# A two-layer graph kernel whose instructions are issued in a second hand-fixed order

## Chip, core and metric

The kernel runs on one core of one Trainium2 chip. The metric is the device time of one launch in microseconds (us). The core has engines that run side by side and each take their instructions in order: PE (TensorE, the matrix products; PEld is its weight load), DVE (VectorE), ACT (ScalarE), POOL (GpSimd) and SP (SyncE, which here issues all transfers). Products land in PSUM, everything else lives in SBUF.

## What is computed

There are 64 independent graphs of 256 nodes with 256 features, each with a 256x256 integer adjacency matrix. Each goes through two layers. Cut to what matters:

```python
# layer 0: attention with 8 heads of 32, masked by relation r = 0..3
q, k = src @ Wq + bq, src @ Wk + bk
attn = softmax(einsum('bhid,bhjd->bhij', q, k) / sqrt(dh))
for r in range(4):
    out += einsum('bhij,bhjd->bhid', attn * (adj == r), src @ Wv[r] + bv[r])
x = ln(src + out @ Wo + bo)
x = ln(x + gelu(x @ W1 + b1) @ W2 + b2)
# layer 1: two graph-attention products, then a feed-forward part
def gat(h, W, a):
    Wh = h @ W
    e = leaky_relu(Wh @ a[:F] + (Wh @ a[F:]).T)
    return softmax(where(adj > 0, e, NEG), axis=1) @ Wh
h = ln(x + gat(gat(x, gW1, ga1), gW2, ga2))
return ln(h + relu(h @ w_ff1 + b_ff1) @ w_ff2 + b_ff2)
```

All products are in f32.

## The kernel before

One graph is cut into 203 named steps. `operations` of the class Graph returns them as a table from name to function. A table `PLACES` gives each name a number; step n of graph g stands at g * PERIOD + PLACES[n], with PERIOD = 60. At the end of the kernel all steps of all graphs are put in one list, sorted by that number, and issued in that order (lines 678 to 690):

```python
plan += [(g * PERIOD + t, i, ops[n]) for i, (n, t) in enumerate(PLACES.items())]
...
for _, _, f in sorted(plan, key=lambda p: p[:2]):
    f()
```

So the numbers are not times. They only set in which order each engine gets its instructions. Since a graph's places stretch over some 408, seven graphs are in flight at a time: while one graph's scores are made, an older one is in its feed-forward part. The 49 remaining weight loads stand at PLACES["jT"] + 3 i (LOAD_STEP), and three pieces that prepare weights at FFA_PLACE, GAT_PLACE and FFB_PLACE.

The steps of a graph, with their engines (m is the half of the heads, 0 or 1; h the head in it; c or the last digit a half of the nodes or a part):

- SP: `load` (features and adjacency), `jT` (transposing load), `eW`/`eR` (softmax weights of one head written to DRAM and read back transposed), `aW`/`aR`, `hW`/`hR`, `bW`/`bR` (the same for the input of the first feed-forward part, of the graph attention, of the second feed-forward part), `y` (residual), `store`.
- PE: `qk0 qk1` (queries and keys), `s0 s1` (scores: 32-row products, four on the array side by side), `v00 v01 v10 v11` (values for four relations), `po0 po1` (masked weights times values: 32-column products, four side by side), `wo`, `au0..3` and `ad0..7` (first feed-forward part up and down), `ga0 ga1`, `ipA ipB` (short products that spread a column), `h10 h11`, `h2`, `bu0..3` and `bd0..7` (second feed-forward part).
- ACT: `qkc` (copy of queries and keys), `exp`, `nrm`, `ec` (copy of a head's weights into PSUM), `oT` (copy of po), `ax` (gelu after au), `bx` (relu after bu), `ln`, `gac`, `zA zB`, `zeA zeB`, `h1c`.
- DVE: `xT`, `max`, `rec`, `vc` (v plus bias), `eT`, `pm` (three relations' masks times weights), `ya`, `aT`, `hT`, `bT`, `ae`, `be`, `st`, `nb`, `zl zm zx zd`, `h2a`.
- POOL: `cast`, `mask0..4`, `pl` (mask of the last relation times weights), `rt`, `ag ar bg br`, `lg lb`, `yb`.

Buffers go by tags. `qk`, `v`, `po`, `wo`, `au`, `bu`, `ga`, `ip`, `h1` and `h2` all take their PSUM tile from the tag mm with two buffers (lines 109 and 116), the down products and `ec` have one buffer each (line 111), and each head of `s` has one (line 110). `pm` and `pl` have four buffers, an eT read three.

In the middle of the run the order of one period is, on PE (cyclic; steps of five graphs):

```
ad2 ad3 ad4 ad5 ad6 ad7 qk1 po1 s0 v10 wo bu0 bu1 bu2 bu3 v11 bd0 ga0 ga1 bd1 ipA
bd2 v00 bd3 bd4 bd5 po0 s1 h10 h11 au0 ipB bd6 bd7 au1 v01 au2 ad0 ad1 au3 h2 qk0
```

on ACT:

```
ec13 nrm03 exp13 qkc0 exp11 ln3 exp10 nrm11 ec02 qkc1 nrm13 oT1 ec01 ln2 nrm12 ec00 bx0
bx1 ln4 bx2 nrm10 exp02 bx3 ln1 ec03 gac0 gac1 ec11 zA exp01 exp03 exp00 nrm02 zeA oT0
nrm01 h1c0 h1c1 zB ax0 ec10 ax1 zeB ax2 ec12 nrm00 ax3 exp12
```

and on SP:

```
store jT eW01 eW00 eR01 eR00 bW bR y load eW03 eR03 hW hR eW11 eR11 aW aR eW12 eR12 eW10
eR10 eW13 eW02 eR13 eR02
```

Of the kernel before, what the change touches and what calls it, by code (L numbers as in the profile page):

```python
# [25 lines left out]

PERIOD = 60.0
PLACES = {
    "load": 12.69, "cast": 34.43, "xT": 36.95, "qk0": 57.08, "jT": 61.53, "qkc0": 62.55, "qk1": 67.8,
    "qkc1": 70.21, "s0": 70.47, "max02": 72.23, "exp02": 81.06, "max01": 82.27, "max03": 86.02,  # L30
    "max00": 88.95, "rec02": 89.87, "exp01": 91.67, "v00": 92.06, "exp03": 92.94, "rec03": 93.5,
    "exp00": 93.85, "nrm02": 93.87, "s1": 95.88, "mask0": 96.09, "rec01": 96.51, "rec00": 97.66,
    "vc00": 97.9, "nrm01": 98.6, "eT02": 98.81, "mask1": 101.7, "max12": 103.23, "eW02": 104.42,
    "v01": 106.53, "max13": 109.53, "eT01": 110.69, "vc01": 112.14, "mask4": 115.25, "nrm00": 115.76,
    "mask2": 116.32, "exp12": 117.58, "eR02": 118.03, "max11": 118.71, "nrm03": 120.47, "eW01": 121.68,
    "exp13": 121.99, "eT00": 122.41, "eW00": 123.28, "max10": 123.96, "eT03": 124.13, "exp11": 124.37,
    "eR01": 124.69, "rec11": 124.91, "exp10": 125.28, "nrm11": 125.32, "rec12": 125.99, "rec13": 126.63,
    "ec02": 126.77, "eR00": 126.89, "eT11": 128.18, "y": 130.66, "nrm13": 131.27, "v10": 131.71,
    "pm02": 131.73, "ec01": 132.85, "mask3": 132.88, "pl02": 133.27, "vc10": 133.65, "pm01": 133.94,
    "nrm12": 134.13, "ec00": 134.17, "rec10": 134.86, "eW03": 135.24, "pl00": 135.39, "eT12": 136.41,  # L40
    "eR03": 136.43, "eW11": 138.29, "pl01": 138.69, "pm00": 140.86, "nrm10": 140.96, "v11": 141.16,
    "vc11": 142.32, "eR11": 143.59, "ec03": 145.79, "pm03": 145.85, "eT10": 146.5, "eT13": 148.99,
    "eW12": 150.09, "ec11": 150.62, "pl03": 151.26, "eR12": 152.59, "po0": 155.58, "oT0": 157.09,
    "eW10": 157.11, "pm11": 157.99, "eR10": 160.55, "eW13": 162.85, "pl11": 163.84, "ec10": 166,
    "pm10": 170.09, "pl10": 170.24, "ec12": 172.37, "yb": 172.85, "eR13": 175.34, "pm12": 178.71,
    "pl12": 179.18, "ec13": 180.43, "pm13": 182.8, "pl13": 184.21, "po1": 189.19, "oT1": 192.18,
    "wo": 192.72, "ya": 194.55, "st1": 197.35, "rt1": 197.54, "nb1": 201.83, "ln1": 203.94, "aT": 203.97,
    "aW": 208.22, "aR": 209.8, "au0": 219.72, "ax0": 225.43, "au1": 226, "ag": 226, "ar": 226.9,
    "ax1": 227.05, "au2": 229.76, "ad0": 230.11, "ax2": 231.84, "ad1": 233.09, "au3": 233.11, "ax3": 236.44,
    "ad2": 240.24, "ad3": 240.48, "ad4": 240.68, "ad5": 240.9, "ad6": 241.73, "ad7": 243.34, "ae": 247.23,  # L50
    "st2": 247.9, "rt2": 249.32, "nb2": 252.05, "ln2": 253.74, "lg2": 255.16, "lb2": 255.29, "hT": 255.42,
    "hW": 256.6, "hR": 258.07, "ga0": 265.07, "ga1": 265.22, "gac0": 266.18, "gac1": 267.17, "ipA": 268.92,
    "zA": 270.83, "zlA": 271.44, "zmA": 272.81, "zxA": 274.65, "zeA": 276.11, "zdA": 277.61, "h10": 278.15,
    "h1c0": 279.36, "h11": 279.54, "h1c1": 279.92, "ipB": 280.31, "zB": 281.13, "zlB": 281.58,
    "zmB": 283.67, "zxB": 284.08, "zeB": 290.21, "zdB": 293.16, "h2": 293.21, "h2a": 300.38, "st3": 301.14,
    "rt3": 303.61, "nb3": 304, "ln3": 304.93, "bT": 306.81, "bW": 308.89, "bR": 309.2, "bu0": 314.34,
    "bu1": 315.21, "bx0": 315.73, "bx1": 317.62, "bu2": 318.08, "bu3": 318.55, "bx2": 318.88, "bx3": 322.44,
    "bd0": 324.24, "bd1": 327.98, "bd2": 330.87, "bd3": 332.25, "bd4": 332.79, "bd5": 333.36, "bg": 335.88,
    "bd6": 340.88, "br": 341.18, "bd7": 342.49, "be": 349.69, "st4": 354.87, "rt4": 359.05, "nb4": 373.16,
    "ln4": 378.29, "lg4": 386.9, "lb4": 395.75, "store": 420.32,  # L60
}
LOAD_STEP = 3.0
FFA_PLACE, GAT_PLACE, FFB_PLACE = 195.0, 200.0, 255.0

# [653 lines left out]
```

## Time and profile before

| what | us |
|---|---|
| median of 3 runs | 3654.48 (3651.39 to 3654.7) |
| the profiled execution | 3653.86 |
| its span, first to last instruction | 3652.1 |
| PE busy in the span | 3567.7 |
| transfers, share of the DMA engines' time | 42.5% |

A matmul record's duration reaches past the start of the next record, since products are pipelined. What a product costs PE is therefore read from the starts of two records in a row, and a wait shows where a row of the timeline carries an idle time and a releaser in square brackets. Every f32 product shows as two records; so a step like au0 (two blocks, each summed over two halves) has eight. Names in the profile are those of tiles: ffa_ps is au, ffa_po is ad, ffb_ps is bu, ffb_po is bd, ga_wps is ga, ga_ips and gb_ips are ipA and ipB, h_ps is h1 and h2.

### The profile page before, as it was taken

The page shows a single profiled execution, that of the slowest core. Times are in us where ns is not written, and L with a number is a line of the kernel's source. Part 1 is how long each engine was busy: PE and PEld are TensorE (multiplying, and loading weights), DVE is VectorE, ACT ScalarE, POOL GpSimd, SP SyncE. Part 2 cuts the span into 40 slices and gives each one's busy share as a digit, 9 for nine tenths or more (in the row PEclk, how much of TensorE's full clock was granted, in tenths as well). Part 3 has the DMA queues.
Part 4 walks back from the last instruction along what each step waited for, and adds up shares of the span by engine and source line. Part 5 has one row for each costly group of instructions (what it writes and reads, how often), then busy time and mean ns, then how long its engine had stood idle before and what let it go on. Part 6 is the DMA issues. An engine that isn't in the chain of part 4 may idle for free.

```text
span 3652.1 us, 65487 instructions
## 1 busy us (share of the span) xinstructions
PE 3567.7 (98%) x22872; PEld 2712.3 (74%) x22872; DVE 2703.1 (74%) x5132; ACT 2630.4 (72%) x6787; POOL 2012.5 (55%) x1734
## 2 busy tenths in 40 slices
PE   6899999999999999999999999999999999999996
PEld 3677777777777777777777777777777777777775
DVE  5777777777777777777777777777777777777762
ACT  4677777777777777777777777677677677777763
POOL 3455555555555555655655655655655655555552
PEclk8999999999999999999999999999999999999998
DMA  7444444444444444444444444444444444444430
GB/s 186 123 128 126 123 135 125 122 132 125 128 128 128 128 126 124 131 125 128 128 127 125 128 129 123 132 126 126 132 125 124 133 124 124 131 126 124 129 96 26
DMA packets 809850, 457.46 MB, mean 125 GB/s; under 512 B 334256, under 2 KB 718896, under 8 KB 809520
## 3 DMA queue, kind: packets, MB, share of 16 engines
q1 hardware_dynamic: 809520, 453.27, 42.5%
q8 instruction: 181, 2.97, 0.4%
q14 instruction: 149, 1.22, 0.1%
HBM read 243.42 MB, written 201.33 MB: 122 GB/s over the span
## 4 chain that ended last, share of the span: by engine, by line
PE 94%; DMA 3%; DVE 1%; ACT 1%; SPq 1%; issue 0%; POOL 0%; POOLq 0%; ACTq 0%; DVEq 0%
PE po L504 12%; PE ffb_ps L349 12%; PE ffb_po L363 12%; PE ffa_ps L349 12%; PE v_ps L436 12%; PE ffa_po L363 12%; PE qk_ps L417 6%; PE s L452 4%; PE h_ps L583 3%; PE ga_wps L534 3%; PE h_ps L597 3%; PE wo_ps L524 3%; DMA eT_d<-eT_sq 1%; DMA hT<-hT_d 0%; PE gb_ips L546 0%
## 5 line engine op out<-in xcount | busy, mean ns | idle before, releaser
L487 DVE TENSOR_TENSOR pm<-rel,pe 128x1536 f32<-128x1536 uint8 x512 | 890.1, 1739 | 137.2 <-PE po L504 118.8
L492 POOL TENSOR_TENSOR pl<-rell,eT 128x512 f32<-128x512 bf16 x512 | 596.4, 1165 | 513.3 <-PE po L504 398.3
L318 POOL TENSOR_TENSOR rs_x<-ve_x,nhalf 128x2 f32<-128x2 f32 x256 | 180.2, 704 | 976.0 <-DVE ve_x L314 686.2
L436 PE MATMUL v_ps<-wv,xT 128*128 128x512 f32 x1024 | 493.2, 604 | 4.5 <-DVE v L443 3.6
L363 PE MATMUL ffb_po<-f,ffb_h 128*128 128x256 f32 x2048 | 493.5, 379 | 0.0
L349 PE MATMUL ffa_ps<-ffa_T,w 128*128 128x256 f32 x2048 | 483.9, 379 | 3.5 <-ACT ffa_h L356 2.5
L465 ACT ACTIVATE e<-s,nmax 128x256 f32<-128x256 f32 x1024 | 474.4, 483 | 3.9 <-DVE nmax L457 1.9
L349 PE MATMUL ffb_ps<-ffb_T,f 128*128 128x256 f32 x2048 | 458.0, 382 | 16.0 <-DMA ffb_T<-ffb_T_d 16.0
L483 ACT COPY pe<-eT 128x512 f32<-128x512 f32 x512 | 306.8, 599 | 227.2 <-DVE pm L487 166.6
L475 ACT ACTIVATE e<-e,rden 128x256 f32<-128x256 f32 x1024 | 466.4, 512 | 0.9 <-DVE rden L470 0.9
L363 PE MATMUL ffa_po<-w,ffa_h 128*128 128x256 f32 x2048 | 462.9, 379 | 0.0
L363 PEld LDWEIGHTS ffb_po<-f,ffb_h 128*128 128x128 f32 x2048 | 379.7, 190 | 98.1 <-issue 57.8
L349 PEld LDWEIGHTS ffa_ps<-ffa_T,w 128*128 128x128 f32 x2048 | 388.9, 190 | 84.1 <-ACT ffa_h L356 18.0
L349 PEld LDWEIGHTS ffb_ps<-ffb_T,f 128*128 128x128 f32 x2048 | 393.0, 192 | 71.4 <-issue 12.4
L443 DVE TENSOR_TENSOR v<-v_ps,bv_r 128x512 f32<-128x512 f32 x256 | 174.3, 681 | 349.0 <-PE v_ps L436 218.4
L363 PEld LDWEIGHTS ffa_po<-w,ffa_h 128*128 128x128 f32 x2048 | 389.5, 190 | 52.5
L269 DVE STREAM_TRANSPOSE eT_sq<-e 128x512 f32<-128x512 f32 x512 | 357.5, 698 | 19.4 <-DMA eT_d<-eT_sq 10.8
L504 PE MATMUL po<-pm,v 128*32 128x256 f32 x6144 | 361.2, 383 | 10.5 <-DVE pm L487 6.5
L457 DVE TENSOR_REDUCE nmax<-s 128x2 f32<-128x512 f32 x512 | 345.1, 675 | 6.2 <-PE s L452 6.2
L504 PEld LDWEIGHTS po<-pm,v 128*32 128x32 f32 x6144 | 187.3, 110 | 167.6 <-ACT pe L483 19.9
L436 PEld LDWEIGHTS v_ps<-wv,xT 128*128 128x128 f32 x1024 | 188.1, 191 | 165.9 <-issue 146.4
L356 ACT ACTIVATE ffb_h<-ffb_ps,bf_c 128x256 f32<-128x256 f32 x512 | 215.0, 473 | 109.4 <-PE ffb_ps L349 109.3
(109 smaller groups left out, 5964.9 us busy)
## 6 DMA issues: line engine op xcount, KB each, us to landing
eT_d<-eT_sq SPq DMA_DIRECT2D x512, 256.0 KB, 3.2
eT<-eT_d SPq DMA_DIRECT2D x512, 256.0 KB, 2.9
xin<-in_x_dram SPq DMA_DIRECT2D x256, 64.0 KB, 3.0
adi<-in_adj_dram SPq DMA_DIRECT2D x64, 256.0 KB, 3.4
y<-in_x_dram SPq DMA_DIRECT2D x64, 256.0 KB, 3.4
ffa_T_d<-ffa_T_sq SPq DMA_DIRECT2D x64, 256.0 KB, 2.4
ffa_T<-ffa_T_d SPq DMA_DIRECT2D x64, 256.0 KB, 3.0
hT_d<-hT_sq SPq DMA_DIRECT2D x64, 256.0 KB, 2.4
```

The lines of the kernel that those rows point to most:

```text
L269: nc.vector.transpose(self.sq.rearrange("p a c k y -> p (c k) a y"), src.rearrange("p c (k a x) -> p (c k) a x", k=KD, a=A))
L349: nc.tensor.matmul(p[:, f - f0, :], self.wa[:, k, f * P:(f + 1) * P], self.x.nodes(k), start=(k == 0), stop=(k == KD - 1))
L363: nc.tensor.matmul(self.p[:, c, :], self.h[:, f, c * P:(c + 1) * P], self.wb[:, f, :], start=(f == 0), stop=(f == KF - 1))
L417: nc.tensor.matmul(p[:, i, :], w[:, k, m * P:(m + 1) * P], self.xT[:, k, :], start=(k == 0), stop=(k == KD - 1))
L436: nc.tensor.matmul(p, self.xT[:, k, jc * P:(jc + 1) * P], wv[:, k, m].rearrange("p r n -> p (r n)"), start=(k == 0), stop=(k == KD - 1))
L457: nc.vector.tensor_reduce(self.nmax[m, h], self.s4[m][h].rearrange("p (c n) -> p c n", c=C), AX.X, ALU.max, negate=True)
L465: nc.scalar.activation(e[:, ic, :], self.s4[m][h][:, ic * N:(ic + 1) * N], AF.Exp, bias=self.nmax[m, h][:, ic:ic + 1], accum_out=self.den[ ...
L475: nc.scalar.activation(e[:, ic, :], e[:, ic, :], AF.Copy, scale=self.rden[m, h][:, ic:ic + 1])
L483: nc.scalar.copy(self.pe[m, h], self.et[m, h].t.rearrange("p b c k y -> p (b c k y)"))
L487: nc.vector.tensor_tensor(self.pm[m, h], self.rel.rearrange("p r b c k y -> p r (b c k y)"), bc(self.pe[m, h], [P, R - 1, C * N]), ALU.mult)
L492: nc.gpsimd.tensor_tensor(self.pm_l[m, h], self.rel_l.rearrange("p b c k y -> p (b c k y)"), self.et[m, h].t.rearrange("p b c k y -> p (b ...
L504: nc.tensor.matmul(po[hp, :], self.v[m][:, jc, r, hp], w, start=(r == 0 and jc == 0), stop=(r == R - 1 and jc == C - 1))
```

## The change

Only numbers change: every value of PLACES, and the places of the three pieces that prepare weights. The functions, buffers, PERIOD and LOAD_STEP stay. Cut to lines that hold steps spoken of below:

```diff
 PERIOD = 60.0
 PLACES = {
-    "load": 12.69, "cast": 34.43, "xT": 36.95, "qk0": 57.08, "jT": 61.53, "qkc0": 62.55, "qk1": 67.8,
-    "qkc1": 70.21, "s0": 70.47, "max02": 72.23, "exp02": 81.06, "max01": 82.27, "max03": 86.02,
...
-    "eW12": 150.09, "ec11": 150.62, "pl03": 151.26, "eR12": 152.59, "po0": 155.58, "oT0": 157.09,
...
-    "bu1": 315.21, "bx0": 315.73, "bx1": 317.62, "bu2": 318.08, "bu3": 318.55, "bx2": 318.88, "bx3": 322.44,
...
-    "ln4": 378.29, "lg4": 386.9, "lb4": 395.75, "store": 420.32,
+    "load": 61.156, "cast": 68.883, "xT": 73.774, "qk0": 86.76, "jT": 88.45, "qkc0": 88.619,
+    "mask4": 89.575, "s0": 102.101, "qk1": 105.137, "qkc1": 105.256, "mask0": 109.639, "max01": 114.685,
+    "max00": 120.08, "v00": 120.331, "exp01": 123.175, "mask1": 125.837, "max03": 126.261, "rec01": 128.358,
...
+    "eR11": 182.108, "ec11": 183.982, "pl03": 184.802, "eT12": 185.247, "eT10": 186.427, "po0": 189.362,
...
+    "bx0": 345.721, "bu1": 345.759, "bu2": 345.86, "bx1": 347.952, "bx2": 349.145, "bd0": 349.451,
+    "bu3": 352.411, "bd1": 356.357, "bd2": 357.761, "bx3": 359.63, "bd3": 365.276, "bd4": 366.983,
...
+    "store": 475.787,
 }
 LOAD_STEP = 3.0
-FFA_PLACE, GAT_PLACE, FFB_PLACE = 195.0, 200.0, 255.0
+FFA_PLACE, GAT_PLACE, FFB_PLACE = 233.0, 237.0, 297.0
```

Sorted, one period of the new order is on PE:

```
v00 bd3 bd4 bd5 po0 bd6 h10 h11 v01 bd7 ipB au0 s1 au1 au2 au3 ad0 qk0 ad1 ad2 ad3
ad4 h2 ad5 ad6 ad7 v10 po1 s0 wo qk1 bu0 bu1 bu2 v11 bd0 ga0 ga1 bu3 ipA bd1 bd2
```

on ACT:

```
exp01 ec11 zeA exp03 oT0 exp00 h1c0 h1c1 exp02 nrm03 ec13 zB nrm00 ax0 nrm02 ax1 nrm01
ax2 ec10 ax3 zeB qkc0 ec12 exp11 exp10 nrm11 ln4 exp13 ln3 exp12 ec00 ln2 oT1 nrm13 ec01
nrm10 qkc1 bx0 bx1 bx2 ec02 nrm12 gac0 ec03 gac1 ln1 zA bx3
```

and on SP:

```
load eW13 eR11 eR13 aW aR y eW12 eW10 eR12 eR10 jT eW00 eW03 eW01 eR00 eW02 eR01 bW eR02
bR eW11 hW hR eR03 store
```

On DVE the stretch that follows h2 in the new order is zdB, pm12, rec11, max12, h2a, st3, max13, eT02, ae, nb3, st2, rec13, bT. At the beginning, 22 weight loads and the inputs of graph 1 stand on SP ahead of the first eW of graph 0; before, 15 weight loads and the same inputs stood there. A graph's places stretch over some 415 now.

## Prediction

> **What bounds the kernel now.** I read the page first: how busy the engines are, and who owns the chain that ended last.
>
> ```profile
> PE 3567.7 (98%) x22872; PEld 2712.3 (74%) x22872; DVE 2703.1 (74%) x5132; ACT 2630.4 (72%) x6787; POOL 2012.5 (55%) x1734
> PE 94%; DMA 3%; DVE 1%; ACT 1%; SPq 1%; issue 0%; POOL 0%; POOLq 0%; ACTq 0%; DVEq 0%
> ```
>
> PE (TensorE) carries the chain; every other engine has a quarter of its time free. The second view is the table by stretches: span, PE busy, PEld, DVE, ACT, POOL, clock, DMA.
>
> ```profile
> 0.00:57.00 57.00, 31.77 (x134) 16.81 (x138) 23.86 (x42) 22.29 (x66) 17.28 (x20) 0.79 0.75 188
> 57.00:114.00 57.00, 44.46 (x330) 28.81 (x322) 37.39 (x61) 30.58 (x87) 22.61 (x19) 0.85 0.57 167
> 457.00:1027.00 570.00, 569.16 (x3698) 433.70 (x3697) 435.87 (x831) 421.98 (x1091) 323.13 (x278) 1.00 0.44 128
> 3592.00:3652.10 60.10, 33.54 (x137) 27.20 (x135) 12.28 (x34) 15.78 (x38) 14.66 (x13) 0.80 0.09 26
> ```
>
> Three stages: a fill with idle PE and a low clock, a middle in which PE is never free, and an emptying end. In the middle I took the starts of the product ipB of successive graphs from the timeline: 50 of 60 intervals are 55.06 us within 0.02, and the sixty come to 3306.8. So a graph costs 55.06 us of PE, and a new order can change only (a) what PE itself spends at borders between kinds of product, (b) waits, (c) fill and end. Third, PE's timeline, for (a); columns are start, duration, line, operation.
>
> ```profile
> 2004.57 1.03 PE L417 MATMUL qk_ps<-xT,wk 128*128 128x256 f32 x4
> 2005.53 2.80 PE L504 MATMUL po<-pm,v 128*32 128x256 f32 x48
> 2008.14 1.04 PE L504 MATMUL po<-pl,v 128*32 128x256 f32 x16
> 2009.12 1.15 PE L452 MATMUL s<-kT,qT 32*128 32x256 f32 x16
> 2010.20 1.98 PE L436 MATMUL v_ps<-wv,xT 128*128 128x512 f32 x4
> 2012.02 1.89 PE L524 MATMUL wo_ps<-wo,oT 128*128 128x256 f32 x8
> ...
> 3483.97 5.34 PE L363 MATMUL ffa_po<-w,ffa_h 128*128 128x256 f32 x24
> 3489.24 2.80 PE L504 MATMUL po<-pm,v 128*32 128x256 f32 x48
> 3492.84 1.98 PE L436 MATMUL v_ps<-wv,xT 128*128 128x512 f32 x4
> 3494.66 1.89 PE L524 MATMUL wo_ps<-wo,oT 128*128 128x256 f32 x8
> ...
> 12.97 1.03 PE L417 MATMUL qk_ps<-xT,wk 128*128 128x256 f32 x4
> 13.92 1.15 PE L452 MATMUL s<-kT,qT 32*128 32x256 f32 x16
> 15.00 1.99 PE L436 MATMUL v_ps<-wv,xT 128*128 128x512 f32 x4
> ```
>
> Starts count here, since durations overlap. An ordinary 256-column record takes 0.2157 us from start to start (24 in 5.18), a 512-column one 0.429, and a group of four small-array records (128*32 or 32*128) also 0.2157. What is above that lies at the borders. Last, ACT behind PE, for (b):
>
> ```profile
> 2039.57 0.38 PE L546 MATMUL gb_ips<-ident,gb_wh 128*128 128x128 f32 x2
> 2040.05 0.84 ACT L553 ACTIVATE gb_z<-gb_ips,gb_wh 128x256 f32<-128x256 f32 x2 [1.63 <-PE gb_ips L546]
> ...
> 167.36 0.84 ACT L356 ACTIVATE ffa_h<-ffa_ps,b_c 128x256 f32<-128x256 f32 x2
> 168.25 1.98 PE L436 MATMUL v_ps<-wv,xT 128*128 128x512 f32 x4 [0.16 <-ACT ffa_h L356]
> ```
>
> ACT starts 0.48 us after an ip product starts; PE starts 0.05 us after the ACT pair that frees its PSUM buffer ends, and then v needs 1.98 where 1.88 is usual, because the weight load was held back too.
>
> **What the Trainium skill says.** "TensorEngine Tiling (Array Packing)", section Key Properties: "Changing tiling mode (not just tile) drains the TensorE". The trace agrees and gives the price, below. "DMA: Bandwidth & Descriptors", section Two DMAs through the same engine are not ordered: a read of what another DMA wrote must wait for that DMA's completion semaphore. The trace shows these waits on the SP queue: 855.2 us over 386 waits of eT reads for eT writes. "Perfetto Trace Analysis", section Identifying the Most-Contended Engine, warns that matmul busy time says little of a distance to peak; hence starts, not the 98%.
>
> **The change, part by part.** Only the order of issue changes: no instruction is added or removed, and per graph the instructions stay the same.
>
> 1. *Borders on PE.* Before, both po stand directly ahead of an s: (po1 s0), (po0 s1). From the rows: into po 0.95−0.86 = 0.09, po 3.59−3.45 = 0.14 over, s 1.08−0.86 = 0.22 over, the next v 1.82−1.72 = 0.10 over: 0.55 us per pair. After, po1 s0 stays, but po0 stands alone between bd5 and bd6, and s1 alone between au0 and au1. Po alone: 5.27−5.18 = 0.09, 3.60−3.45 = 0.15, 0.10: 0.35. S alone: 0.95−0.86 = 0.09, 0.22, 0.10: 0.41. Together 0.75 against 0.55: +0.20 us per graph, on the path since PE never rests. Times 62 graphs: +12.3 us.
>
> 2. *A new wait: v00 for bx3.* All wide products share two PSUM buffers (tag mm), so a product waits for the reader of the product two before it. After, the run is bu3, ipA, v00, with bd1 and bd2 (not in mm) between ipA and v00. ACT's order there is ln1, zA, bx3. Count from the start of ipA: zA starts at 0.48, its two instructions take 0.72 before the next can start (2026.41 to 2027.13 for ga_z), the bx3 pair 0.84: 2.04, plus 0.05 to PE = 2.09. PE would be ready at 0.22 + 8×0.2157 = 1.95. So 0.14 waiting and 0.10 for the held-back weights: 0.25 us. Before, bu3 was followed by v11 and ga0 and nobody waited. Sixty graphs: +15.0 us. Behind v00 on PE stands everything. From below 0 (if the buffers are not used in strict turn), from above about 0.5 (if ln1, just ahead, is late); I take 0.25.
>
> 3. *Other short waits.* I set PE densely and put the traced durations of each engine behind it in the new order. The distance from h2 to bu0 falls from 16.9 to 12.9 us of PE work (before: qk0, six ad, qk1, po1, s0, v10, wo; after: three ad, v10, po1, s0, wo, qk1). Between lie h2a, st3, rt3, nb3, ln3, bT, bW, bR; in the empty machine this takes 9.86 us (3615.11 to 3624.97). In the after order pm12 and max12 are done before h2a, while max13, eT02, ae and st2 share DVE with it: I get 11.1 to 11.5. SP's eW02, eR01 and eR02 stand ahead of bW and bR but are ready earlier. It fits with 1.4 us to spare: 0, above 1 us a graph. The hT read gains (it came late in six graphs before, worth most of the 3.2 us by which sixty intervals exceed 60×55.06): −2. aR→au0 has 28 us instead of 24. ACT switches between the exp and gelu tables twice a graph instead of four times, 2.6 us of ACT at 1.283 each; PE does not wait for ACT there, so 0. The tight readers of PSUM (gac0, h1c0, vc00, vc01) have 0.1 to 0.25 us left: 0.
>
> 4. *Fill.* Before, ipB of graph 0 starts at 164.7, with 102.4 us of PE work ahead of it: 62.3 lost. SP decides it: its queue holds the 49 weight loads (0.45 to 0.7 us each), the input loads and the transposing loads, and each eR waits about 3.2 us for its eW. Before, the first four writes and reads of graph 0 come in pairs spread to 48.8, and po0.0 goes on at 54.3, po1.0 at 75.2. After, more loads (22) stand ahead of the first write: end of the first transposing load 13.1, loads 13.5, inputs 3.5, second transposing load 2.5, about 33 instead of 26.4; but then eW00, eW03, eW01 go out together and four reads are out by about 44. That gives po0.0 at about 49 and po1.0 at 68. Going on the same way: au0.0 at 99 instead of 107.8, ga0.0 at 131 (with a wait of 2.6 for hT) instead of 148.7, ipB.0 at 147. So −17.7 if nothing else interferes; such a walk forgets waits, the low clock among them. I take −13, between −5 and −18.
>
> 5. *End.* After the last po1 both orders hold the same products, and the same two waits rule (h2→bu 9.9, ipA→h10 6.9 us). Interval by interval I get 135.1 us for the last three against 134.9, and a tail 0.6 shorter: 0, within ±3.
>
> Sum: 12.3 + 15.0 − 2 − 13 = +12.3 on the profiled run's own 3653.86 us (span 3652.1): 3666. The median of the runs shown is 3654.48, so this is +0.3% against it.
>
> **Rivals.** *A, the forecast:* 3666, own range 3655 to 3682 (fill −18 to −5, v00 0.15 to 0.45). For it: both terms come from rows, and PE has no slack. Chance 0.52.
> *B, not slower:* the wait of v00 does not arise because it gets ipA's buffer, which zA frees 0.73 us before bx3 frees bu3's; the code says only that two buffers share a tag. Then 3666 − 15 = 3651. It decides if the buffer is free before 1.95 us after ipA starts. With a longer fill gain this is faster than before. Chance 0.27.
> *C, clearly slower:* bR lands after PE has come to bu0. The before trace shows ffb_T waits only in the end stage, at 16.9 us distance; at 12.9 it needs 1.4 us more queueing than I found on SP, DVE or ACT. 0.5 us a graph gives 3696, 1 us gives 3726. Chance 0.15.
> *D, the order matters only at the two ends:* border costs overlap with something and the wait is absent; fill −17.7 gives 3636. Against it: the gaps lie in the starts of the records. Chance 0.06.
>
> **How the numbers follow.** About 0.2% (7.3 us) is what a measurement here can tell from no change, so "same" is 3647 to 3662. A gives 0.42 slower, 0.08 same, 0.02 faster; B 0.03, 0.14, 0.10; C 0.15 slower; D 0.06 faster. Slower 0.60, same 0.22, faster 0.18. Range 3643 to 3697: D and the best of B lie below, the worse half of C above.
>
> **What would show it.** ipB intervals of 55.5 us: 55.26 says no v00 wait, 56 or more says C. PE idle ahead of v_ps with ACT ffb_h as releaser, some 60 times at 0.15 us; po followed by ffb_po with a first step of 0.31. ipB.0 near 152. Gelu and exp table loads halved. I am wrong if ffb_ps, h_ps or ga_wps waits for DMA or DVE in most graphs, or if the fill loses time.

## The result, and where the time went

The kernel after takes 3664.13 us (median of 11 runs, 3662.32 to 3670.3), the kernel before 3655.03 in the same comparison (11 runs): a ratio of 1.0027, interval 1.0017 to 1.0036. The profiled execution of after, 3670.3 us with a span of 3668.5, is the slowest of its eleven. So the two profiles differ by 16.4 us where the medians differ by 9.1; this matters below, where single profiles are compared.

The page of after, the lines for engines, for the chain that ended last, and the groups of the two products that the prediction had an eye on:

```profile
PE 3585.4 (98%) x22872; PEld 2714.5 (74%) x22872; DVE 2748.4 (75%) x5132; ACT 2509.6 (68%) x6661; POOL 2004.0 (55%) x1734
...
PE 94%; DMA 2%; DVE 2%; SPq 1%; issue 0%; ACT 0%; POOL 0%; POOLq 0%; ACTq 0%; DVEq 0%
...
L352 PE MATMUL ffb_ps<-ffb_T,f 128*128 128x256 f32 x2048 | 470.1, 383 | 25.8 <-DMA ffb_T<-ffb_T_d 25.8
L439 PE MATMUL v_ps<-wv,xT 128*128 128x512 f32 x1024 | 485.3, 597 | 5.2 <-ACT oT L513 4.2
```

PE still carries the chain. ACT has 126 instructions fewer and 121 us less busy time: its table loads fall from 255 to 129, two less per graph but for the ends. That is worth nothing here, since PE did not wait for ACT there. In the whole run v_ps never waited for ffb_h, the reader that term 2 was about.

The starts of ipB cut each profiled execution into four parts (us):

| part | before | after |
|---|---|---|
| start to ipB of graph 0 (fill) | 164.7 | 162.5 |
| sixty intervals | 3306.9 | 3320.7 |
| last three intervals | 134.9 | 138.5 |
| from the last ipB to the end | 45.5 | 46.8 |
| usual interval | 55.06 | 55.26 |

Sixty times 0.20 is 12.0 of the 13.8 in the middle; the rest comes from single intervals that are longer than usual, which add 5.1 us after and 3.2 before. After, they are six, 0.6 to 1.3 us too long: in five bu0 stands 0.37 to 1.07 us for ffb_T, in the first au0 stands 0.56 us for a reader on DVE. The 0.20 can be read off PE's timeline of after (start, duration, line, operation):

```profile
2032.22 2.75 PE L366 MATMUL ffb_po<-f,ffb_h 128*128 128x256 f32 x12
2034.90 2.80 PE L507 MATMUL po<-pm,v 128*32 128x256 f32 x48
2037.52 1.05 PE L507 MATMUL po<-pl,v 128*32 128x256 f32 x16
2038.49 1.13 PE L366 MATMUL ffb_po<-f,ffb_h 128*128 128x256 f32 x4
2039.46 1.90 PE L586 MATMUL h_ps<-ga_wh,ga_z 128*128 128x258 f32 x8
...
2044.00 1.89 PE L352 MATMUL ffa_ps<-ffa_T,w 128*128 128x256 f32 x8
2045.82 1.15 PE L455 MATMUL s<-kT,qT 32*128 32x256 f32 x16
2046.90 5.45 PE L352 MATMUL ffa_ps<-ffa_T,w 128*128 128x256 f32 x24
2052.18 1.03 PE L366 MATMUL ffa_po<-w,ffa_h 128*128 128x256 f32 x4
```

From start to start: 2.68 for twelve records that need 2.59 (0.09 into po), 3.59 for po (0.14 over), 0.97 for four records that need 0.86 (0.11 out): 0.34. For s: 1.82 − 1.73, 1.08 − 0.86, 5.28 − 5.18: 0.41. The two alone come to 0.75; the pair before cost 0.55.

The place of term 2, engines together, from ipA on:

```profile
2028.55 0.38 PE L549 MATMUL ga_ips<-ident,ga_wh 128*128 128x128 f32 x2
2028.77 1.89 PE L366 MATMUL ffb_po<-f,ffb_h 128*128 128x256 f32 x8
2029.03 0.84 ACT L556 ACTIVATE ga_z<-ga_ips,ga_wh 128x256 f32<-128x256 f32 x2 [0.35 <-PE ga_ips L549]
2029.76 0.84 ACT L359 ACTIVATE ffb_h<-ffb_ps,bf_c 128x256 f32<-128x256 f32 x2
2030.50 1.88 PE L439 MATMUL v_ps<-wv,xT 128*128 128x512 f32 x4
```

ACT runs as forecast: bx3, the second ACT row, ends at 2030.60, 2.05 after ipA starts. But v00 starts at 2030.50, 1.95 after ipA, exactly when PE is ready, while bx3 still reads its buffer. It has the buffer that zA, the first ACT row, left at 2029.87.

The fill by waits of PE, a selection of rows, first before, then after (engine, line, what it waited for: us in total, times, longest):

```profile
PE po L504 <- DVE pm L487: 6.5, 2, 5.2
PE ga_wps L534 <- DMA hT<-hT_d: 4.5, 1, 4.5
PE v_ps L436 <- DVE v L443: 3.6, 1, 3.6
```

```profile
PE po L507 <- DVE pm L490: 6.8, 3, 3.2
PE v_ps L439 <- ACT oT L513: 4.2, 2, 3.7
PE gu_ps L250 <- DVE gw2T L243: 3.4, 1, 3.4
PE ga_wps L537 <- DMA hT<-hT_d: 2.8, 1, 2.8
```

All rows of this view up to ipB of graph 0 come to 45.3 us before and 39.2 after. The products ahead of that point take an estimated 93.5 and 92.7 us at full-clock steps. The prediction had 102.4 for before. That is what comes out, nearly, when the narrow products of the weight preparation are priced like 256-column ones; but the 32 one-column records at 137.98 of before take 3.49 us to the start of the next product, 0.11 each. So of the time lost in the fill (71.2 and 69.8), waiting gave back 6 us, and what is neither a listed wait nor full-speed work grew from 25.9 to 30.5; products at a low clock are part of it, as the last section shows. The lost time (the start of a step less the full-speed work ahead of it) shows where the gain went:

| lost time at the start of (us; po0.0 is po0 of graph 0) | po0.0 | po1.0 | wo.0 | au0.0 | ga0.0 | ipB.0 |
|---|---|---|---|---|---|---|
| before | 30.0 | 47.7 | 48.1 | 57.7 | 66.6 | 71.2 |
| after | 30.2 | 42.8 | 47.7 | 57.9 | 61.9 | 69.8 |

At po1 of graph 0 after is 4.9 us ahead, one step later nearly level: po1 started on the first masked weights, waited 1.70 us for the next (pm), and then ran 42 of its records in 4.00 us where 42 quarters of 0.2157 make 2.27; the granted clock over 70 to 77 us was 0.52. At ga0 after is ahead again, by 4.8 us, since it waits 1.7 us less for hT and not at all for the buffer of au2, which took 2.5 before; of this 3.4 are lost on the way to ipB, where products run slowly (last section).

### The profile page after: what moved, and what is told of

It is laid out like the page before. It is cut to its first block, busy times and chain, and to the rows that moved or that the text cites. A ratio compares the mean times of both kernels' runs of the same rounds, so it can differ in the third digit from the quotient of the medians.

```text
span 3668.5 us, 65599 instructions
## 1 busy us (share of the span) xinstructions
PE 3585.4 (98%) x22872; PEld 2714.5 (74%) x22872; DVE 2748.4 (75%) x5132; ACT 2509.6 (68%) x6661; POOL 2004.0 (55%) x1734
## 4 chain that ended last, share of the span: by engine, by line
PE 94%; DMA 2%; DVE 2%; SPq 1%; issue 0%; ACT 0%; POOL 0%; POOLq 0%; ACTq 0%; DVEq 0%
PE ffa_ps L352 12%; PE ffb_ps L352 12%; PE ffb_po L366 12%; PE po L507 12%; PE ffa_po L366 12%; PE v_ps L439 11%; PE qk_ps L420 6%; PE s L455 3%; PE ga_wps L537 3%; PE h_ps L586 3%; PE h_ps L600 3%; PE wo_ps L527 3%; DMA ffb_T_d<-ffb_T_sq 1%; DMA ffb_T<-ffb_T_d 1%; SPq L136 1%; DMA eT_d<-eT_sq 0%
## 5 line engine op out<-in xcount | busy, mean ns | idle before, releaser
L352 PE MATMUL ffb_ps<-ffb_T,f 128*128 128x256 f32 x2048 | 470.1, 383 | 25.8 <-DMA ffb_T<-ffb_T_d 25.8
L439 PE MATMUL v_ps<-wv,xT 128*128 128x512 f32 x1024 | 485.3, 597 | 5.2 <-ACT oT L513 4.2
L366 PE MATMUL ffa_po<-w,ffa_h 128*128 128x256 f32 x2048 | 472.7, 379 | 0.0
L352 PE MATMUL ffa_ps<-ffa_T,w 128*128 128x256 f32 x2048 | 469.3, 382 | 0.6 <-DVE v L446 0.6
L352 PEld LDWEIGHTS ffa_ps<-ffa_T,w 128*128 128x128 f32 x2048 | 379.1, 190 | 68.2 <-issue 21.0
L507 PEld LDWEIGHTS po<-pm,v 128*32 128x32 f32 x6144 | 187.7, 110 | 191.7 <-DVE nb_x L325 45.5
L439 PEld LDWEIGHTS v_ps<-wv,xT 128*128 128x128 f32 x1024 | 195.5, 191 | 144.4 <-issue 123.8
```

What stands on the lines that cost most here:

```text
L352: nc.tensor.matmul(p[:, f - f0, :], self.wa[:, k, f * P:(f + 1) * P], self.x.nodes(k), start=(k == 0), stop=(k == KD - 1))
L366: nc.tensor.matmul(self.p[:, c, :], self.h[:, f, c * P:(c + 1) * P], self.wb[:, f, :], start=(f == 0), stop=(f == KF - 1))
L439: nc.tensor.matmul(p, self.xT[:, k, jc * P:(jc + 1) * P], wv[:, k, m].rearrange("p r n -> p (r n)"), start=(k == 0), stop=(k == KD - 1))
L507: nc.tensor.matmul(po[hp, :], self.v[m][:, jc, r, hp], w, start=(r == 0 and jc == 0), stop=(r == R - 1 and jc == C - 1))
```

## The experiments

Each is a change of the numbers that set the order alone; the diffs are cut to the entries that change. The theory: borders between kinds of product set the 0.20 of the middle; v00 does not wait, because it gets the buffer whose reader comes first; the fill follows a stream that waits in several places. The rival for the first is that order matters only at the ends, for the second that buffers go in strict turn, for the third that single waits or SP's queue of weight loads decide.

**1. The border alone, in the kernel before.**

```diff
-    "s1": 95.88,
+    "s1": 99.6,
```

> The kernel before, with one step moved: s1 goes from directly behind po0 to between h11 and au0, so that po0 and s1 each stand alone among full-size products, as in the kernel after; the rest of the order, fill and end stay. Border theory (a drain at every change of product kind, 0.55 us for an adjacent pair against 0.35 + 0.41 apart): ipB intervals go from 55.06 to 55.26 us, the median up by about 12 us (62 x 0.20), to 3667; with 2 us for shifts of waits, 9 to 16. Rival (the gaps between records overlap with something, order matters only at the ends): intervals stay 55.06, time within 3 us of before. If the pair apart costs more than this the theory has mis-sized a border.

3708.07 us, ratio 1.0147 (1.0133 to 1.0161); interval 55.90. Four times too much. The timeline of this run, PE with the readers of po0 and of v00:

```profile
2009.70 1.05 PE L504 MATMUL po<-pl,v 128*32 128x256 f32 x16
2010.89 0.37 ACT L510 COPY oT<-po 128x256 f32<-128x256 f32 x1 [3.07 <-PE po L504]
2010.89 0.69 DVE L443 TENSOR_TENSOR v<-v_ps,bv_r 128x512 f32<-128x512 f32 x1 [2.14 <-PE po L504]
2011.32 2.01 PE L583 MATMUL h_ps<-ga_wh,ga_z 128*128 128x258 f32 x8 [0.57 <-ACT oT L510]
2013.26 1.15 PE L452 MATMUL s<-kT,qT 32*128 32x256 f32 x16
```

From the second part of po to h10 it is 1.62 us where 0.97 is usual: 0.65 lost on oT0, which empties po0's PSUM buffer. s1 needs no buffer of that tag and had stood between them, a cover that the expectation had forgotten. What remains, 0.84 − 0.65 = 0.19, fits the border; experiment 2 shows it without a wait. The rows also bear on term 2: v00, po0, h10 follow each other in the shared tag, so in strict turn h10 would need v00's buffer. It starts at 2011.32, while vc00, the reader of v00, runs until 2011.58. It took po0's buffer, which oT0 left at 2011.26.

**2. The same with another cover.**

```diff
-    "s1": 95.88,            "bd5": 333.36,
+    "s1": 99.6,             "bd5": 335.7,
```

> The kernel before with s1 moved to between h11 and au0 as in the first run of this kind, and in addition bd5 moved from ahead of po0 to between po0 and h10. In that first run the interval was 55.90, and h10 stood 0.57 us for oT0, the copy that frees po0's PSUM buffer. Theory: the isolated s1 costs 0.20 us per graph at the borders, and the other 0.64 was this wait, which s1 had covered; with bd5 (0.86 us) as the new cover the wait goes and the interval is 55.26, the time about 12 us above before (3665 to 3670). Rival (an isolated s costs 0.84 whatever stands behind po0): 55.9, some 53 us above.

Interval 55.26; 3672.29 us, ratio 1.005 (1.0036 to 1.0064). The time is 2 us above the range that was expected: this profile has 140.1 us in its last three intervals against 134.9. The timeline, with bd5 (ffb_po) behind po and s between h11 and au0:

```profile
2039.22 1.05 PE L504 MATMUL po<-pl,v 128*32 128x256 f32 x16
2040.20 1.13 PE L363 MATMUL ffb_po<-f,ffb_h 128*128 128x256 f32 x4
2041.16 1.90 PE L583 MATMUL h_ps<-ga_wh,ga_z 128*128 128x258 f32 x8
2043.00 1.15 PE L452 MATMUL s<-kT,qT 32*128 32x256 f32 x16
2044.07 1.99 PE L349 MATMUL ffa_ps<-ffa_T,w 128*128 128x256 f32 x8
```

No row carries a wait, and the price of taking a pair apart is 0.20 in an order that, but for the cover bd5, is that of before. Order does not matter only at the ends.

**3. The reader of bu3 late, in the kernel after.**

```diff
-    "bx3": 359.63,
+    "bx3": 363.2,
```

> The kernel after, with bx3 placed behind exp01 on ACT (places 359.63 to 363.2), so that the reader of bu3 ends later by at least one exp. If the two PSUM buffers of the shared tag are used in strict turn, v00 must take bu3's buffer and waits for bx3: about 1.7 us more a graph, intervals near 57, some +100 us. If a product gets the buffer that was released first, v00 takes ipA's, freed by zA, and does not notice bx3: intervals 55.26. Then the product after v00 that needs the other buffer (po0, four full-size steps later) is the first that could be late, and it has about 6 us: 0, total -3 to +6 us.

Interval 55.26, 3665.68 us, ratio 1.0032 (1.002 to 1.0044): as after. The timeline from ipA on:

```profile
2025.62 0.38 PE L549 MATMUL ga_ips<-ident,ga_wh 128*128 128x128 f32 x2
2026.10 0.84 ACT L556 ACTIVATE ga_z<-ga_ips,ga_wh 128x256 f32<-128x256 f32 x2 [0.35 <-PE ga_ips L549]
2027.56 1.88 PE L439 MATMUL v_ps<-wv,xT 128*128 128x512 f32 x4
2027.72 0.85 ACT L359 ACTIVATE ffb_h<-ffb_ps,bf_c 128x256 f32<-128x256 f32 x2
```

v00 starts before bx3 has even begun. Strict turn is out.

**4. Both readers late.**

```diff
-    "exp01": 123.175,
+    "exp01": 115.3,
```

> The kernel after with exp01 moved ahead of zA on ACT (place 123.175 to 115.3), so that zA, and bx3 behind it, end about 0.9 us later, both still issued ahead of v00. zA would then end at about 2.22 after the start of ipA and free ipA's buffer at 2.27, bx3 at 3.0, and PE is ready for v00 at 1.95. Theory (v00 gets ipA's buffer, whose reader stands first in the order of issue): v00 waits 0.32 for ga_z and 0.10 for its held-back weight load, interval about 55.7, time some 25 us above after. Rival (strict turn, v00 gets bu3's buffer): it waits for ffb_h until 3.0, interval 56.3 to 56.5, some 65 us above. No wait at all (55.26) would say that the readiness of PE or the start of zA is misread.

Interval 55.26, 3662.88 us, ratio 1.0022 (1.0013 to 1.0032). No wait, so neither the theory nor its rival met the number. The timeline, with ipA's start at 2025.80:

```profile
2026.72 0.84 ACT L556 ACTIVATE ga_z<-ga_ips,ga_wh 128x256 f32<-128x256 f32 x2
2027.44 0.85 ACT L359 ACTIVATE ffb_h<-ffb_ps,bf_c 128x256 f32<-128x256 f32 x2
2027.74 1.88 PE L439 MATMUL v_ps<-wv,xT 128*128 128x512 f32 x4
```

The start of zA was misread: exp01 did not have to wait for ipA, as zA does, so it began 0.02 us after ipA started and zA ended at 1.76, ahead of PE's 1.94. bx3 ended at 2.49, 0.55 after v00 had started, which says the same as experiment 3. What a real wait of v00 for ipA's buffer costs was not measured.

**5. The slack between h2 and bu0, in the kernel after.**

```diff
-    "h2": 331.003, "h2a": 331.095,
+    "h2": 331.95,  "h2a": 332.0,
```

> The kernel after with h2 placed behind ad7 instead of ahead of ad5, so that h2 starts 2.59 us (12 records of 0.2157) later against bu0. The trace of after gives the chain from h2 to the landing of bR some 1.5 us of slack. Theory (the distance of 12.9 us was nearly used up): ffb_ps waits for ffb_T in nearly every graph, about 1.1 us each (0.7 to 1.4), interval 56.0 to 56.7, time 45 to 85 us above after. Rival (the chain is shorter than read, the five late reads of after have another cause): interval 55.26 to 55.4, time within 8 us of after.

Interval 57.17, 3784.66 us, ratio 1.036 (1.0346 to 1.0374): worse than the theory, and not where it said. PE, DVE and ACT in the middle of this run:

```profile
2010.67 0.69 DVE L604 TENSOR_TENSOR ffa_res<-h_ps,ffa_res 128x512 f32<-128x512 f32 x1 [3.46 <-PE h_ps L600]
...
2013.20 0.48 ACT L468 ACTIVATE e<-s,nmax 128x256 f32<-128x256 f32 x1 [4.65 <-DVE nmax L460]
...
2015.87 1.98 PE L455 MATMUL s<-kT,qT 32*128 32x256 f32 x16
...
2017.71 0.65 DVE L446 TENSOR_TENSOR v<-v_ps,bv_r 128x512 f32<-128x512 f32 x1
2018.41 1.99 PE L527 MATMUL wo_ps<-wo,oT 128*128 128x256 f32 x8 [0.56 <-DVE v L446]
...
2021.60 0.65 DVE L531 TENSOR_TENSOR y<-wo_ps,y 128x512 f32<-128x512 f32 x1
2022.30 1.99 PE L352 MATMUL ffb_ps<-ffb_T,f 128*128 128x256 f32 x8 [0.17 <-DVE y L531]
```

DVE takes its instructions in order. It stood 3.46 us for h2 ahead of h2a (the first row), and what stands behind h2a came late: a max, for which exp on ACT waited 4.65 us, vc10 (reader of v10) and ya (reader of wo). They hold PSUM that PE needs next: the score buffers of s, which took 1.98 us instead of 1.15, and the buffers of wo and bu0. From s to wo it is 2.54 us instead of 1.08, of which 0.83 lies inside s, and from qk1 to bu0 2.06 instead of 1.72: 1.80 of the 1.91. The read bR is not the cause: PE's waits for ffb_T in the whole run are 26.7 us, against 25.8 in after. So the landing of bR was not the first thing to run out; the readers of PSUM queued behind h2a were.

**6 to 9. Four edits of the fill.** Third weight preparation ahead of ga0 of graph 0; ec11 behind oT0; fewer weight loads ahead of the first write, in after and in before.

```diff
-FFA_PLACE, GAT_PLACE, FFB_PLACE = 233.0, 237.0, 297.0
+FFA_PLACE, GAT_PLACE, FFB_PLACE = 233.0, 237.0, 289.0
```

> The kernel after, with the third piece of weight preparation (32 one-column products) moved from behind ipA of graph 0 to ahead of ga0 of graph 0 (place 297 to 289), where PE waits 2.85 us for hT in the fill. In the middle nothing moves: intervals 55.26. Theory that the fill lost its gain partly to this piece, which takes 6.8 us of PE at the place that has no wait to hide it: ipB of graph 0 starts 3 to 10 us earlier than 162.5, time lower by the same. Rival (the later chain, not PE, sets ipB of graph 0, or the piece only shifts the low clock elsewhere): ipB within 1 us, time within 2 us of the kernel after (3664).

```diff
-    "ec11": 183.982,
+    "ec11": 190.5,
```

> The kernel after, with ec11 moved behind oT0 on ACT (place 183.982 to 190.5). In the fill ec11 waits for the landing of the read eR11, and oT0 behind it holds the PSUM buffer that v01 of graph 1 needs: PE stands 3.7 us there. Theory (an in-order queue behind a late transfer takes part of the fill gain): that wait goes, ipB of graph 0 3 to 4 us earlier, time lower by 3 to 4 us, intervals stay 55.26. Rival (the next wait, po1 for pm, takes it over, since it waits for the same stream of reads): v01's wait goes but po1 waits that much longer; ipB and time within 1 us of the kernel after.

```diff
-LOAD_STEP = 3.0
+LOAD_STEP = 4.0
```

> The kernel after with LOAD_STEP 4 instead of 3, so that some 16 instead of 22 weight loads stand on SP ahead of the first write of graph 0. Theory (SP's queue decides the fill): the first write goes out some 3 to 4 us earlier, po0 and po1 of graph 0 start 2 to 4 us earlier, ipB of graph 0 2 to 4 us, the time falls by the same, to 3660 to 3662; intervals 55.26. Rival (the softmax of the first graphs and the low clock decide, or a weight now comes too late): po0 and po1 within 1 us, time within 2 us of after, or worse.

> The kernel before with LOAD_STEP 4 instead of 3. The middle stays at 55.06. Theory (SP's queue decides the fill): the fill gets 2 to 4 us shorter, time 3651 to 3653, below both kernels. Rival: within 2 us of before, or later weights are missed and it is slower.

| edit | median | ratio to before | ipB of graph 0 |
|---|---|---|---|
| third preparation earlier | 3663.32 | 1.0026 (1.0016 to 1.0035) | 160.2 |
| ec11 behind oT0 | 3664.83 | 1.0032 (1.002 to 1.0045) | 161.6 |
| fewer loads, after | 3664.21 | 1.0024 (1.0014 to 1.0034) | 158.9 |
| fewer loads, before | 3655.19 | 0.9999 (0.9991 to 1.0008) | 163.9 |

No median moved: the theories of all four miss, and what their rivals said of the time holds. The fill of single profiles can't be read to better than 3 us: in runs 3, 4 and 5, which leave the fill's transfers and weights alone, ipB of graph 0 stands at 159.5, 159.3 and 160.0, against 162.5 in the profile of after. Against these the first three edits gain nothing that single profiles could show. The waits of PE in the fill of the second edit say what happened:

```profile
PE po L507 <- DVE pm L490: 8.7, 4, 5.1
PE gu_ps L250 <- DVE gw2T L243: 5.0, 1, 5.0
PE v_ps L439 <- ACT oT L513: 1.0, 2, 0.6
```

The aimed-at wait fell by 3.2 us, and the two above it rose by 1.9 and 1.6. Fewer loads moved even the beginning of the fill little. In after the first write of graph 0 went out 1.0 us earlier (32.7 against 33.7) and po0 started at 48.2 as it had without the edit. In before the first write went out 1.5 us earlier and po0 started 3.8 us earlier (44.2 against 48.0), but then stood 8.99 us for pm and went on at 53.8 instead of 54.3; ipB came 0.8 us earlier. The number of weight loads ahead of the first write does not decide the fill.

**10. Three of them together, in after.**

```diff
-    "ec11": 183.982,
+    "ec11": 190.5,
-LOAD_STEP = 3.0
-FFA_PLACE, GAT_PLACE, FFB_PLACE = 233.0, 237.0, 297.0
+LOAD_STEP = 4.0
+FFA_PLACE, GAT_PLACE, FFB_PLACE = 233.0, 237.0, 289.0
```

> The kernel after with the three fill edits together: third weight preparation at 289, ec11 behind oT0, LOAD_STEP 4. Each alone took a wait of 2 to 4 us out of the fill and left the median within 1 us. Theory (the fill is elastic: the waits follow one stream of scores, writes and reads, and a wait removed in one place comes back in another or as work at a low clock): ipB of graph 0 between 157 and 161, median within 3 us of after (3661 to 3666). Rival (the edits add up, only the single effects are under the spread): ipB of graph 0 at 152 to 155, median 3654 to 3658.

3660.4 us, ratio 1.0018 (1.0012 to 1.0025), ipB of graph 0 at 155.0. Theory and rival each miss by a little: ipB stands at the edge of what the rival put, the median between the two. That the edits add up in the fill is borne out by experiments 11 and 12, which keep them and have ipB at 155.1 and 157.0, where the profiles of after with one of them or none have 158.9 to 162.5. But the 3.7 us by which the median falls are well short of the waits that they aim at, and how much of this is real is at the limit of what the intervals tell.

**11 and 12. The pair put back, in the order of after with these fill edits.**

```diff
-"max02": 130.375, "exp03": 129.241, "exp00": 131.502, "exp02": 133.214,
-"s1": 140.011, "bd7": 375.366,
+"max02": 126.3, "exp03": 128.0, "exp00": 127.0, "exp02": 129.0,
+"s1": 129.45, "bd7": 378.2,
```

> The kernel of the run before (after with the three fill edits), and s1 put back directly behind po0: s1 140.011 to 129.45, max02, exp00, exp03 and exp02 moved ahead of oT0 so that the score buffers are free by then, and bd7 moved to between au0 and au1, where s1 had been the cover for the buffer au1 and au2 take. Border theory: with (po1 s0) and (po0 s1) adjacent again the interval goes from 55.26 to 55.06, the exact value of before, 12 us off 3660: 3646 to 3650, which is below both kernels. Rival (the slots that come free are needed elsewhere: au2 waits for ax0, h10 for the softmax of ga_z delayed by the exps, or s1 for exp02): interval above 55.26, by about 0.1 to 0.8 us, and time 3660 to 3710.

3701.47 us, ratio 1.0132 (1.0115 to 1.0149), interval 55.89: the rival's outcome, at a place that it had not named. The timeline at the place that bd7 had left:

```profile
2055.51 0.38 PE L549 MATMUL gb_ips<-ident,gb_wh 128*128 128x128 f32 x2
2055.72 0.69 DVE L446 TENSOR_TENSOR v<-v_ps,bv_r 128x512 f32<-128x512 f32 x1 [1.92 <-PE v_ps L439]
2056.46 1.99 PE L352 MATMUL ffa_ps<-ffa_T,w 128*128 128x256 f32 x8 [0.57 <-DVE v L446]
```

From ipB to au0 it is 0.95 us instead of 0.22, and au0 itself takes 0.10 more: 0.83, all of the excess over 55.06. Here au0 has the buffer of v01, the product two before it. The mend:

```diff
-    "bd6": 370.019,
+    "bd6": 375.3,
```

> The run before had every border as planned but one new wait: au0 stood 0.57 us for vc01 (v01's reader on DVE) and lost 0.83 us in all with its held-back weight load, since bd7 no longer stood between v01 and ipB; 55.89 minus 0.83 is 55.06. Here bd6 moves from ahead of h10 to between v01 and ipB (370.019 to 375.3), which puts 0.86 us back there; s1 covers oT0 for h10. Theory: interval 55.06, time 12 us under the 3660 of the three fill edits: 3646 to 3650, below the kernel before by some 6 us (ratio 0.9975 to 0.999). Rival (the cover of 0.14 us left over at au0 is not enough, or h10 now waits): interval 55.1 to 55.9, time above 3652.

Interval 55.06; 3650.64 us (21 runs), ratio to before 0.9986 (0.998 to 0.9993). The last run beats both kernels. PE's timeline of it at the pair that was put back:

```profile
2023.62 1.05 PE L507 MATMUL po<-pl,v 128*32 128x256 f32 x16
2024.60 1.15 PE L455 MATMUL s<-kT,qT 32*128 32x256 f32 x16
2025.67 2.01 PE L586 MATMUL h_ps<-ga_wh,ga_z 128*128 128x258 f32 x8
```

Against before its profile has 7.7 us less in the fill (157.0), 3306.6 in the middle, and 4.4 more in the end. So the gain over before comes from the fill of the new order with its edits; whether the order of before could be given the same fill was not tried.

## Why the prediction was right, and where it was not

The total was right (3666 against 3664.13), but this is in part luck: two of its terms were wrong with opposite signs. With term 2 gone and the fill as it came, the same sum would have given 3653.86 + 12.3 − 2 − 2.3 = 3661.9. Short waits that grew instead of shrinking (about 4 us) and the end (4.9) lead from there to the profiled 3670.3. The median lies 6 us under that execution; the profiles of experiments 3 and 4, which are near it in time, are 3 us shorter in the fill and 2 to 3 us shorter in the end.

1. *Borders, +12.3:* right, and shown by undoing and doing it. Intervals of 55.06 (before), 55.26 (after), 55.26 (experiment 2) and 55.06 (experiment 12) follow the pairs alone, and 55.26 is the figure that the prediction gave for its borders without term 2. What the Trainium skill says in "TensorEngine Tiling (Array Packing)", section Key Properties, of a drain at a change of mode agrees with where the price falls, at the changes between 128\*128, 128\*32 and 32\*128. The size, 0.34 to 0.55 us, is this trace's; that it is the drain that costs it, no run shows by itself.

2. *A new wait, v00 for bx3, +15.0:* this step failed. ACT's times were right (bx3 ended at 2.05 us where 2.04 was forecast), but "a product waits for the reader of the product two before it" is not how the two buffers are given out. Experiments 1, 3 and 4 exclude strict turn. What fits all the rows shown is that a product takes the buffer whose reader stands first in the order of issue. For v00 this is ipA's (zA ahead of bx3), for h10 in experiment 1 that of po0, the product just before (oT0 ahead of vc00), for au0 in experiment 11 that of v01, two before (vc01 ahead of zB). No run turned one of these readers round to test the rule. Rival B had named the mechanism for v00, though not the total of 3651, since its fill fell short too. 0 us in place of 15.0.

3. *Other short waits, −2:* wrong in size and sign, by little. PE's waits for hT fell from 6.0 to 2.8 us in the whole run, as said. But its waits for ffb_T rose from 16.0 to 25.8: 3.1 us of this in five graphs of the middle, where bR landed after PE had come to bu0, and the other 6.7 in the end. What the sixty intervals hold above the usual went from 3.2 to 5.1, the five graphs making 4.3 of it. The shortened distance from h2 to bu0 thus cost something in five graphs of the middle and nothing in the others there. That more would have been expensive is shown by experiment 5, though through readers of PSUM behind h2a and not through rival C's late read.

4. *Fill, −13:* failed. −2.3 in the profiled execution, and about −5 by the profiles of experiments 3, 4 and 5. The forecast for po0.0 (49, measured 48.2) and po1.0 (68, measured 70.3) was good, and so was the wait of ga0 for hT (2.6, measured 2.85). The failing part was "going on the same way" from there: from po1 to ipB its own figures lose 13.8 us (68 − 27.5 is 40.5, 147 − 92.7 is 54.3), where before had lost 23.5 and after lost 27.0. Most of it was gone by au0, which stood at 108.8 where 99 was forecast. The loss of that stretch could be read in the trace of before, and it was larger there than the sum took it to be: the 62.3 us lost before rest on too dear a price for the narrow products and are about 71. A start that comes earlier was taken for an end that comes earlier.

5. *End, 0 ± 3:* +4.9 in the profiled execution (3.6 in the last three intervals, 1.3 in the tail), outside; in experiments 3 and 4, with 135.9 and 136.6 us for the last three intervals and tails of 46.7 and 47.0, it is +2 to +3. PE's listed waits from the start of ipB of graph 60 on come to 26.2 us before, 30.0 after and 29.4 in experiments 3 and 4, but to 25.7 in experiment 2, which has the order of before but for s1 and bd5. So about 3 us of waiting belong to the new order, and "the same two waits rule" missed their size: bu alone waits 22.7 us for ffb_T where it had waited 16.0. Other waits of before (h10 for ga_wh) shrank. The rest of the end varies: experiment 2, without more waiting, ends 5 us later than before, and why stays open.

Rival D, that order matters only at the two ends, falls with experiment 2: the borders alone move the middle by 0.20 us a graph.

## What to carry to other kernels

When one engine never rests, price every change of kind between its neighbouring instructions from the starts in its own timeline, and then ask of each instruction that is moved which buffer it had been covering: experiments 1 and 11 lost 0.65 and 0.83 us a period on a cover that was forgotten, more than the border at stake. Ask also what stands behind the moved step on an engine that takes its work in order: experiment 5 lost 1.91 us that way. Find out from the trace, not from a rule of turn, which buffer a product waits for; one row in which a product starts while the supposed reader still runs is enough. In a fill, carry the traced losses of every later stretch over to the new order before crediting an early start; here po1 started 4.9 us earlier and then waited for the next piece of the same stream.

## What was not expected of the hardware

The 32 one-column products of the third weight preparation ran 6.83 us in after and 3.63 in before, and the products behind them ran slowly too: the four records of v took 3.76 us where 1.88 is usual. The granted clock fits this: it was 0.50 from 142 to 155 us of after, the stretch in which these products stand (143.8 to 154.1). Before had a like stretch, 0.51 from 143 to 153, but PE stood idle in 4.5 us of it, waiting for hT, and its 32 products had come ahead of it, at 138.0. So a wait taken out of the fill can come back in part as slower products; no run isolated what sets these stretches or what they cost in all.

A wait costs more than the idle time in its row. In experiment 11 the row shows 0.57 us and the place lost 0.83. Of the difference 0.10 lies inside the product that follows, and 0.16 is the reach of ipB's record (0.38) past its usual distance to the next start (0.22), which the idle time leaves out.
